# One table set for exp and log, the logarithm summed by TensorE, and two more products per pass on GpSimd, in a bidirectional Mamba layer

## The chip, the cores and the metric

The kernel runs on one core of a Trainium2 chip. The metric is the device time of one execution in microseconds (us). The engines are called as in the profile: PE (TensorE, with PEld for its weight loads), DVE (VectorE), ACT (ScalarE), POOL (GpSimd) and SP (SyncE, which issues most of the DMAs). Each engine takes its instructions in the order in which they were written; between engines semaphores keep the order.

## The reference

One image of 64x64 positions and 256 channels, all in float32. Layer 0 is a convolution block with attention, layer 1 takes the 4096 positions as a sequence: layer norm, a Mamba layer forwards and one backwards, their sum `m`, a layer norm and a small two-layer network on it, and then a mixture of experts. The change lies in the Mamba layers:

```
xz = x @ in_proj.T;  xc, z = split(xz)               # 512 channels each
xc = silu(conv4(xc) + conv_b)
dt, B, C = split(xc @ x_proj.T)                       # 16 columns each
dt = softplus(dt @ dt_proj.T + dt_b)                  # 512 channels
h  = exp(dt * A) * h + dt * B * xc                    # 512 channels x 16 states, along 4096 positions
y  = (sum over states of h * C) + xc * Dp
out = (y * silu(z)) @ out_proj.T
m = fwd + bwd;   t = x1 + m + mlp(layer_norm(m))       # x1 is layer 1's input before its layer norm
```

## The kernel before

The Mamba stage (`mamba_phase`) cuts the 4096 positions into 8 chunks of N = 512 and handles the two directions by turns: 16 *passes*, pass i being chunk i // 2, forwards where i is even and backwards where it is odd. A pass has 32 *slots*, numbered 0 to 31 (`at` in the code): 4 groups of 128 channels (e), 4 groups of states (k) and two halves (j = 0, 2). A slot works on tiles of 128 partitions x 1024. The order of all engines is written out by hand in one loop over 512 slots n (L1979); nothing reorders it.

What a slot n issues, in this order:

- `inflow(n + 2)`, POOL: `dbx` = dt*xc times B (L1890). Three buffers.
- `keep(n - 1)`, ACT: the last column of the states is kept for the next chunk (L1934).
- `decay(n + 1)`, ACT: two Exp of 128x512 into `da` in PSUM (L1880). Two buffers.
- `bring(n + 1)`, ACT or POOL: adds what is carried in from the chunk before.
- `recur(n)`, DVE: the scan along 1024 columns (L1903) in place in `da`, and the product with C (L1908) from `da` to the SBUF tile `h`. Four buffers of `h`. In the slots of the set `POOLED` the scan writes to `h` at once, and POOL does the product in place one slot later (`pooled`, L1913).
- `sum_states`, PE: four matmuls that add up the states of two slots into the PSUM tile `y` (L1943). The pair (n, n + 1) is summed in slot n + 2, or in slot n + 3 where slot n is in `POOLED`. With each new e a matmul for xc * Dp comes first (L1941).
- At slots 0, 8, 16 and 24, `close`, DVE: `y` times silu(z) (L1952).

Beside the slots run *generators*, one step per slot:

- `prepare(q)` makes what pass q needs. It begins in slot 27 of pass q - 2 and lies mostly in pass q - 1: `in_proj` of xc (L1339), the convolution as matmuls with diagonal weights (`taps`, L1385, slots 3 to 6), Silu of xc (slot 8, L1389), the projection to dt, B and C (`wx`, L1394, slot 9), the projection of dt (`wdt`, L1414, slots 11 to 14) with Abs and Relu on ACT, Exp (slot 16, L1417), then in slots 17 to 22 three identity matmuls that add the rounding error, exp(-|.|) and the Relu part (L1430) and a copy by ACT; in slot 23 Ln (L1434) and two matmul groups of z; in slots 24 to 29 and in slots 2 and 4 of the next pass the steps of `dt_piece` on POOL: v = 0 adds Ln to dt (L1458), v = 1 multiplies by xc (L1469) and writes both to DRAM, from where they are read back spread over partitions.
- `output(i - 1)`, slots 1 to 3: the out projection of the pass before (L1527), copied or added into `m`.
- `tail(c)`, one for each chunk but the last: layer norm of `m`, `m + x1` on POOL (L1550), up-projection (L1558), the leaky step (ACT L1562, DVE L1564), down-projection in two halves (L1569, L1574), and another layer norm. Each step names the engine that it needs first, and is taken only in slots that are not in that engine's set in `FULL`. A tail begins in slot 26 of an even pass and ends in slot 25 of the next even pass; the last ends in slot 31 of pass 15. It has one PSUM buffer (`tl_psum`).

The matmul results of `prepare` and `output` share two PSUM buffers (`mm_psum`). ACT needs a table load whenever a function outside the loaded set comes: Silu and Exp do, and Ln was loaded from a set of its own, so a pass has six loads: two for Silu of xc and back, two for Ln and back, two for silu(z) at slot 0 (L2019) and back.

`start()` does for pass 0 what `prepare` does for the others, in part on DVE. After the loop, `ending()` finishes the last chunk.

Of the kernel before, what the change touches and what calls it, by code (L numbers as in the profile page):

```python
# [14 lines left out]
FP = mybir.dt.float32  # L15
# [9 lines left out]
P = 128  # L25
# [1230 lines left out]
def mamba_phase(cx, early, w_in, w_x, w_out, w1, w2, x1d, ud, bcd, dtd, x2d, u2d, usum):  # L1256
# [12 lines left out]
    with ExitStack() as ctx:  # L1269
# [59 lines left out]

        def mm_psum():  # L1330
            return pmm.tile([P, N], FP, name="mm", tag="mm")
# [19 lines left out]
        def in_pair(q, e):  # L1351
            return [in_proj(q % 2, gots[q]["u"], e), in_proj(q % 2, gots[q]["u"], e + 1)]

        def few():
            return sp.tile([P, N], FP, name="few", tag="few", bufs=3)

        def prepare(q):
# [31 lines left out]
            nc.scalar.activation(xc, xc, AF.Silu)  # L1389
            yield  # L1390
            ps = mm_psum()
            nx = DR + 2 * DS
            for e in range(ET):
                nc.tensor.matmul(ps[0:nx, :], wx[d][:, e, :], xc[:, e, :], start=e == 0, stop=e == ET - 1)  # L1394
            yield
            xd = few()[0:nx, :]
            nc.scalar.copy(xd, ps[0:nx, :])

# [7 lines left out]
            for e in range(ET + 1):  # L1406
                if e > 0:
                    ex = early.wide("ex")[:, :, 0:N] if e == 1 else ex
                    dt = dt or sp.tile([P, ET, N], FP, name="dt", tag="dt")
                    nc.scalar.activation(ex[:, e - 1, :], ps, AF.Abs, bias=cx.col(f"dtb{d}", e - 1))  # L1410
                    nc.scalar.activation(dt[:, e - 1, :], ps, AF.Relu, bias=cx.col(f"dtb{d}", e - 1))
                if e < ET:
                    ps = mm_psum()
                    nc.tensor.matmul(ps, wdt[r, P * e : P * e + P], xd[r, :], start=True, stop=True)  # L1414
                yield
# [4 lines left out]
            for e in range(ET + 2):  # L1420
                if e < ET:
                    rd = rds[e] = few()
                    nc.scalar.activation(rd, ex[:, e, :], AF.Identity, scale=-1.0, bias=-1.0)
                    nc.scalar.add(rd, rd, 1.0)
                if e > 1:
                    nc.scalar.copy(dt[:, e - 2, :], sums.pop(e - 2))
                if 0 < e <= ET:
                    ps = sums[e - 1] = mm_psum()
                    for v, x in enumerate((rds.pop(e - 1), ex[:, e - 1, :], dt[:, e - 1, :])):
                        nc.tensor.matmul(ps, cx.ident, x, start=v == 0, stop=v == 2)  # L1430
                yield


            nc.scalar.activation(ex, ex, AF.Ln, bias=1.0)  # L1434
            zs = in_pair(q, ET)
            yield
            got["dt"] = dt
            for at, (v, e) in enumerate(((0, 0), (1, 0), (0, 1), (0, 2), (0, 3), (1, 1))):
                if at == 3 and q > 1:
                    load_first(q, 0)  # L1440
                dt_piece(q, v, e, ex)
                if at in (0, 2):
                    z = sp.tile([P, 2, N], FP, name="z", tag="z", bufs=3)
                    got.setdefault("z", []).append(z)
                if at < 4:
                    nc.scalar.copy(z[:, at % 2, :], zs[at % 2])  # L1446
                if at == 1:
                    zs = in_pair(q, ET + 2)
                    if q + 1 < 2 * NCH:
                        load_u(q + 1)  # L1450
                yield

        def dt_piece(q, v, e, ex=None, eng=nc.gpsimd):


            dt, xc = gots[q]["dt"], gots[q]["xc"]
            if v == 0:
                eng.tensor_tensor(dt[:, e, :], dt[:, e, :], ex[:, e, :], ALU.add)  # L1458
                if q < 2:
                    return  # L1460
                if e == 0:
                    firsts[q] = ip.tile([P, ET], FP, name="first", tag="first", bufs=1)
                nc.gpsimd.tensor_tensor(firsts[q][:, e : e + 1], dt[:, e, 0:1], odd[:, 0:1], ALU.add)
                if e % 2:
                    first_rows[q, e // 2] = cx.rows.tile([P, 2], FP, name="first_row", tag="first_row", bufs=2)
                    nc.sync.dma_start(out=first_rows[q, e // 2], in_=firsts[q][:, e - 1 : e + 1])
            else:
                x = few()
                eng.tensor_tensor(x, dt[:, e, :], xc[:, e, :], ALU.mult)  # L1469

                eng.tensor_tensor(dt[:, e, 0:1], dt[:, e, 0:1], odd[:, 1:2], ALU.add)
                for w, piece in enumerate((dt[:, e, :], x)):
                    nc.sync.dma_start(out=dtd[2 * q + w][e].rearrange("p j n -> (p j) n"), in_=piece)
# [63 lines left out]
        def tail(c):  # L1537
# [3 lines left out]
            yield from layer_norm(cx, tl, tl_psum, m, hn, nc.gpsimd, 2)  # L1541
            x1 = tl.tile([P, CT, N], FP, name="x1", tag="ln_xc")
            nc.sync.dma_start(out=x1, in_=x1d[c])
            for t in range(CT):
                nc.scalar.activation(
                    hn[:, t, :], hn[:, t, :], AF.Identity, scale=cx.col("lng", t), bias=cx.col("lnb", t)
                )
            yield "DMA"
            yield "POOL"
            nc.gpsimd.tensor_tensor(m, x1, m, ALU.add)  # L1550
# [33 lines left out]
        def start():  # L1584
# [10 lines left out]
            nc.scalar.activation(xc, xp[:, :, 0:N], AF.Silu)  # L1595
            for d in range(2):
                nc.scalar.activation(aneg[d], cx.col(f"alog{d}", 0, ET * DS), AF.Exp)

                nc.vector.tensor_scalar(aneg[d], aneg[d], -1.0, -1e-30, ALU.mult, ALU.min)
# [78 lines left out]
            for z in got["z"]:  # L1678
                nc.scalar.activation(z, z, AF.Silu)
            dt_piece(0, 0, 3, ex)  # L1680
# [188 lines left out]
        firsts, first_rows, got_first, brought = {}, {}, {}, {}  # L1869
# [80 lines left out]
        def close(i, e):  # L1950
# [7 lines left out]
        POOLED = {4, 10, 12, 18, 28}  # L1958
# [7 lines left out]
            "PE": {0, 1, 2, 3, 4, 5, 6, 7, 9, 18, 19, 20, 21, 23, 24, 25, 27, 29},  # L1966
            "ACT": {0, 6, 7, 8, 9, 16, 17, 18, 19, 20, 21, 22, 23, 30, 31},
            "POOL": {0, 1, 2, 4, 24, 25, 26, 27, 28, 29, 30, 31},
# [4 lines left out]
        with tc.manual_schedule(engines=ORDERED):  # L1973
# [5 lines left out]
            for n, (i, e, k, j) in enumerate(slots):  # L1979
# [37 lines left out]
                if at == 0 and i > 0:  # L2017
                    for z in gots[i]["z"]:
                        nc.scalar.activation(z, z, AF.Silu)  # L2019
                if i == 0:  # L2020
                    step(begin)
# [4 lines left out]
                if i > 0 and at in (2, 4):  # L2026
                    dt_piece(i, 1, 2 if at == 2 else 3)
# [7 lines left out]
                for _ in range(1 + (i == 2 * NCH - 1 and at in (4, 6, 7))):  # L2035
                    if tails and (i == 2 * NCH - 1 or at not in FULL[needs[0]]):
                        needs[0] = next(tails[0], None)
                        if needs[0] is None:
                            tails.pop(0)
                            needs[0] = "PE"  # L2040
# [358 lines left out]
```

## Time and profile before

| | us |
|---|---|
| median of 3 runs (lowest to highest) | 4099.89 (4095.22 to 4108.44) |
| profiled execution: its time / its span | 4114.01 / 4112.1 |
| Mamba stage in it, first scan to the end of the last slot | 1946.9 to 3819 |
| busy over the span: PE, DVE, ACT, POOL | 3586.2, 3503.9, 2667.8, 1836.6 |
| granted clock of PE over the span | 0.918 |
| passes 2 to 14, scan of slot 0 to the next pass's | 113.5 to 119.8 each |

A line of the groups reads: source line, engine, operation, output <- inputs, shape and count | busy us, mean ns of one | idle time of the engine just before, and what ended most of it. In a timeline a line begins with start and duration in us; the idle time before it stands in brackets. Matmuls of float32 are recorded in two records each. A line of the waits has the waiting instruction, the one that released it, the sum in us, how often, and the longest. A line by stretches has the stretch, its length, the busy time (and count) of PE, PEld, DVE, ACT and POOL, PE's granted clock, the DMA share and GB/s.

### The profile page before, as it was taken

To read this page: it belongs to the slowest core of one execution; us is meant where nothing else is said; L and a number is where in the kernel's file an instruction comes from. 1 tells how busy PE (TensorE), PEld (TensorE's weight loads), DVE (VectorE), ACT (ScalarE), POOL (GpSimd) and SP (SyncE) were. 2 spreads that over 40 slices of the span, in tenths; PEclk is the share of its full clock that TensorE was granted. 3 is DMA by queue.
4 is the path that set the end of the run, shared out by engine and by line. 5 is a ranking of instruction groups with operands and counts; after the bars stand their busy time and mean duration, and the time that the engine had idled before them with its cause. 6 is when DMAs were issued, how large, how long until landed. Compare 5 with 4: busy or idle time off the path is not lost. (4 is left out here: it accounts for less than half of the span.)

```text
span 4112.1 us, 43244 instructions
## 1 busy us (share of the span) xinstructions
PE 3586.2 (87%) x14792; PEld 1183.0 (29%) x14792; DVE 3503.9 (85%) x2919; ACT 2667.8 (65%) x4152; POOL 1836.6 (45%) x1284
## 2 busy tenths in 40 slices
PE   6769888999999999998888788888888888876898
PEld 2324332222222222222222222222223232222444
DVE  8998877989889889877899999999999999999322
ACT  1111226988887878876777777778787777775222
POOL 3020000000000000001888889888888989888100
PEclk9889998999999999998888998898899899888999
DMA  6232215223322223214334344344333434332221
GB/s 208 93 98 95 81 59 157 51 60 65 65 56 62 63 54 65 58 42 122 118 106 129 116 124 130 121 119 129 113 113 119 144 109 133 117 122 90 64 62 55
DMA packets 164324, 399.93 MB, mean 97 GB/s; under 512 B 36997, under 2 KB 46469, under 8 KB 163838
## 3 DMA queue, kind: packets, MB, share of 16 engines
q1 hardware_dynamic: 137166, 304.26, 24.0%
q0 software_dynamic: 24624, 84.43, 8.9%
q10 hardware_dynamic: 2304, 8.39, 0.6%
q8 instruction: 118, 1.93, 0.2%
q14 instruction: 112, 0.92, 0.1%
HBM read 268.17 MB, written 79.56 MB: 85 GB/s over the span
## 5 line engine op out<-in xcount | busy, mean ns | idle before, releaser
L1890 POOL TENSOR_TENSOR dbx<-dtxr,b 128x1024 f32<-128x1024 f32 x512 | 1202.9, 2360 | 201.9 <-DVE da L1903 80.2
L1044 ACT ACTIVATE e<-sc 128x1024 f32<-128x1024 f32 x1024 | 993.8, 1023 | 178.5 <-PE sc L1037 152.7
L1903 DVE TENSOR_TENSOR_SCAN da<-da,state,dbx 128x1024 f32<-128x1024 f32 x432 | 1013.9, 2347 | 16.9 <-ACT da L1880 7.2
L954 DVE TENSOR_TENSOR s<-s,e 128x1024 f32<-128x1024 f32 x768 | 880.5, 1216 | 25.1 <-ACT e L1044 24.4
L1880 ACT ACTIVATE da<-dtr,aneg 128x512 f32<-128x512 f32 x1024 | 708.2, 692 | 33.2 <-DMA dtr<-dtd 3.7
L1037 PE MATMUL sc<-q,kS 32*128 32x512 f32 x4096 | 652.8, 650 | 15.6 <-ACT e L1044 11.4
L961 PE MATMUL av<-e,vT 128*32 128x512 f32 x4096 | 557.2, 612 | 0.4 <-ACT e L1044 0.4
L1908 DVE TENSOR_TENSOR h<-da,c 128x1024 f32<-128x1024 f32 x432 | 529.1, 1225 | 33.2 <-PE y L1943 1.2
L977 POOL DMA_DIRECT2D s<-s x94 | 81.5, 874 | 953.0 <-DVE s L954 901.7
L1943 PE MATMUL y<-h,sel 128*32 128x512 f32 x2048 | 368.9, 654 | 99.2 <-DVE h L1908 74.7
L462 PE MATMUL cv<-v,u 128*128 128x512 f32 x928 | 414.9, 607 | 28.7 <-DVE v L286 13.3
L1037 PEld LDWEIGHTS sc<-q,kS 32*128 32x128 f32 x4096 | 211.5, 185 | 460.0 <-issue 259.4
L1339 PE MATMUL mm<-u,win 128*128 128x512 f32 x464 | 252.8, 695 | 77.1 <-ACT z L1446 25.8
L462 PEld LDWEIGHTS cv<-v,u 128*128 128x128 f32 x928 | 179.4, 195 | 261.9 <-issue 228.4
L560 DVE SCALAR_TENSOR_TENSOR acc<-pad,wdw_s,acc 128x768 f32<-128x768 f32 (+1 forms) x192 | 236.0, 1234 | 19.9 <-ACT acc L553 14.2
L1934 ACT COPY state<-da 128x2 f32<-128x2 f32 x431 | 67.9, 158 | 264.6 <-DVE h L1908 263.5
L1385 PE MATMUL mm<-xp,taps 128*128 128x512 f32 x480 | 212.8, 595 | 0.0
L143 POOL TENSOR_TENSOR ln_few<-ln_few,minus_half 128x4 f32<-128x4 f32 x29 | 34.8, 1201 | 397.5 <-DMA ln_few<-ln_row 259.6
L954 DVE TENSOR_TENSOR s<-e 128x1024 f32<-128x1024 f32 x128 | 151.9, 1217 | 62.2 <-ACT e L1044 53.5
L1903 DVE TENSOR_TENSOR_SCAN h<-da,state,dbx 128x1024 f32<-128x1024 f32 x80 | 187.5, 2344 | 13.0 <-ACT state L1934 11.7
L961 PEld LDWEIGHTS av<-e,vT 128*32 128x32 f32 x4096 | 82.0, 108 | 400.5 <-issue 390.3
L1913 POOL TENSOR_TENSOR h<-h,c 128x1024 f32<-128x1024 f32 x80 | 188.4, 2355 | 1.0 <-ACT state L1934 1.0
(379 smaller groups left out, 3940.9 us busy)
## 6 DMA issues: line engine op xcount, KB each, us to landing
dtr<-dtd SPq DMA_DIRECT2D x128, 512.0 KB
dtxr<-dtd SPq DMA_DIRECT2D x128, 512.0 KB
s<-s POOLq DMA_DIRECT2D x94, 512.0 KB, 5.9
b<-bcd SPq DMA_DIRECT2D x64, 256.0 KB
c<-bcd SPq DMA_DIRECT2D x64, 256.0 KB
dtd<-dt SPq DMA_DIRECT2D x64, 256.0 KB
dtd<-few SPq DMA_DIRECT2D x64, 256.0 KB
u<-uv SPq DMA_DIRECT2D x24, 640.0 KB
```

The costliest lines, as they stand in the source:

```text
L462: nc.tensor.matmul(rows4(ps), u[:, dy, P * ci : P * ci + P], v[:, dy : dy + HR, ci, :], start=dy + ci == 0, stop=dy == k - 1 and ci == CT - 1,
L560: nc.vector.scalar_tensor_tensor(o, src, w_ap, o, ALU.mult, ALU.add)
L954: nc.vector.tensor_tensor(z, x, y, ALU.add)
L961: nc.tensor.matmul(g.av[32 * h : 32 * h + 32, :], vT[:, kb, P * t + 32 * h : P * t + 32 * h + 32], es[h // 2][:, h % 2, :], start=kb == 0, ...
L1037: nc.tensor.matmul(ps[h // 2][:, h % 2, :], kS[r, t, P * kb : P * kb + P], q_t[r, t, :], start=True, stop=True,)
L1044: nc.scalar.activation(e, ps[i], AF.Exp)
L1339: nc.tensor.matmul(ps, win[d][:, t, P * e : P * e + P], u[:, t, ::-1] if d else u[:, t, :], start=t == 0, stop=t == CT - 1,)
L1880: nc.scalar.activation(da[:, v, :], dts[i, e, j][0][:, v, :], AF.Exp, scale=aneg[i % 2][:, a : a + 1])
L1890: nc.gpsimd.tensor_tensor(u, dts[i, e, j][1], bcs[i, k][0][:, None, :].to_broadcast([P, 2, N]), ALU.mult)
L1903: nc.vector.tensor_tensor_scan(das[n].rearrange("p v n -> p (v n)"), da.rearrange("p v n -> p (v n)"), u.rearrange("p v n -> p (v n)"), st ...
L1908: nc.vector.tensor_tensor(h, da, bcs[i, k][1][:, None, :].to_broadcast([P, 2, N]), ALU.mult)
L1943: nc.tensor.matmul(ys[i, e][32 * j : 32 * j + 32, :], cx.sel, hs[n + j // 2][:, j % 2, :], start=False, stop=k == SQ - 1,)
```

## The change

- ACT loads the set that holds Exp and Ln together after each Silu (`exp_and_log`), so Ln needs no load: four loads per pass.
- Ln is taken in four parts (`logs`). The sum of dt in PSUM stays open after its three identity matmuls, and a fourth adds Ln. ACT copies the finished sum (`keep_dt`) and, for the carry, its first column. The v = 0 steps on POOL go, but for `start()`; the four v = 1 steps lie in slots 21, 23, 25 and 27.
- The four projections of z go from slots 23 and 25 to slots 9, 10, 19 and 21, their copies to 10, 11, 20 and 22.
- The tail adds x1 to `m` by two identity matmuls for each half and a copy by ACT, within the waits of its first layer norm, instead of on POOL.
- `POOLED` is {0, 4, 8, 12, 16, 20, 28} instead of {4, 10, 12, 18, 28}.
- `FULL` is changed. By the order of the new instructions a tail now begins in slot 8 of an even pass and ends in slot 30 of the next odd pass: up-projections in slots 23, 25, 28 and 30 of the even pass, the two halves of the down-projection in slots 8 and 10 of the odd one. The last ends in slot 17 of pass 15.

```diff
+        def exp_and_log():
+            nc.scalar.preload_act_table_set("natural_log_exp_and_others")
...
             nc.scalar.activation(xc, xc, AF.Silu)
+            exp_and_log()
             yield
...  (wx)
+            z_of(q, 0)
             yield
             xd = few()[0:nx, :]
             nc.scalar.copy(xd, ps[0:nx, :])
+            keep_z(q, 0)
+            z_of(q, 1)
...  (Exp)
+            def keep_dt(e):
+                nc.scalar.copy(dt[:, e, :], sums[e])
...
+                nc.scalar.copy(firsts[q, h][:, e % 2 : e % 2 + 1], sums[e][:, 0:1])
...
+            rounding(0)
+            yield
+            for e in range(ET + 1):
+                if e > 0:
+                    keep_dt(e - 1)
                 if e < ET:
-                    rd = rds[e] = few()
...
+                    total(e)
+                if e < ET - 1:
+                    rounding(e + 1)
+                if 0 < e < 3:
+                    keep_z(q, e + 1)
                 yield
-            nc.scalar.activation(ex, ex, AF.Ln, bias=1.0)
-            zs = in_pair(q, ET)
...
+                if e < ET:
+                    logs(e)
+                    if e < 2:
+                        z_of(q, e + 2)
+                    nc.tensor.matmul(sums[e], cx.ident, ex[:, e, :], start=False, stop=True)
+                if e > 0:
+                    dt_piece(q, 1, e - 1)
...
                 yield
...  (tail)
-            yield from layer_norm(cx, tl, tl_psum, m, hn, nc.gpsimd, 2)
-            x1 = tl.tile([P, CT, N], FP, name="x1", tag="ln_xc")
+            x1 = tl.tile([P, CT, N], FP, name="x1", tag="a1b")
             nc.sync.dma_start(out=x1, in_=x1d[c])
+            for need in layer_norm(cx, tl, tl_psum, m, hn, nc.gpsimd, 2):
...
+                if waits > 1:
+                    nc.scalar.copy(m[:, waits - 2, :], ps)
+                if waits < 3:
+                    ps = tl_psum()
+                    nc.tensor.matmul(ps, cx.ident, m[:, waits - 1, :], start=True, stop=False)
+                    nc.tensor.matmul(ps, cx.ident, x1[:, waits - 1, :], start=False, stop=True)
...
-            nc.gpsimd.tensor_tensor(m, x1, m, ALU.add)
...
-        POOLED = {4, 10, 12, 18, 28}
+        POOLED = {0, 4, 8, 12, 16, 20, 28}
...
-            "PE": {0, 1, 2, 3, 4, 5, 6, 7, 9, 18, 19, 20, 21, 23, 24, 25, 27, 29},
-            "ACT": {0, 6, 7, 8, 9, 16, 17, 18, 19, 20, 21, 22, 23, 30, 31},
-            "POOL": {0, 1, 2, 4, 24, 25, 26, 27, 28, 29, 30, 31},
+            "PE": {1, 2, 3, 4, 5, 6, 7, 9, 18, 20, 21, 22, 24, 27, 29},
+            "ACT": {0, 6, 7, 8, 9, 14, 15, 16, 20, 22, 30, 31},
+            "POOL": {1, 5, 9, 13, 17, 21, 23, 25, 27, 29, 30, 31},
...
                     for z in gots[i]["z"]:
                         nc.scalar.activation(z, z, AF.Silu)
+                    exp_and_log()
...
-                if i > 0 and at in (2, 4):
-                    dt_piece(i, 1, 2 if at == 2 else 3)
...
-                for _ in range(1 + (i == 2 * NCH - 1 and at in (4, 6, 7))):
+                if tails and (i == 2 * NCH - 1 or at not in FULL[needs[0]]):
...
```

## The prediction

> **What bounds the kernel now.** I read the page's groups first, then the busy times by stretch, the DVE's waits, and the timelines of single slots. "Slot" and "pass" are as in the section on the kernel; times inside a pass are starts of the 512 rows of L1903.
>
> ```profile
> L1890 POOL TENSOR_TENSOR dbx<-dtxr,b 128x1024 f32<-128x1024 f32 x512 | 1202.9, 2360 | 201.9 <-DVE da L1903 80.2
> L1903 DVE TENSOR_TENSOR_SCAN da<-da,state,dbx 128x1024 f32<-128x1024 f32 x432 | 1013.9, 2347 | 16.9 <-ACT da L1880 7.2
> L1908 DVE TENSOR_TENSOR h<-da,c 128x1024 f32<-128x1024 f32 x432 | 529.1, 1225 | 33.2 <-PE y L1943 1.2
> L1913 POOL TENSOR_TENSOR h<-h,c 128x1024 f32<-128x1024 f32 x80 | 188.4, 2355 | 1.0 <-ACT state L1934 1.0
> ```
>
> The Mamba stage runs from the first scan (1946.9) to 3819. By stretches, DVE is busy 1791 of these 1872 us, POOL 1629, PE 1552, ACT 1425: DVE sets the pace. A slot whose product is on DVE lasts 3.52 to 3.59 us from scan to scan; with the product on POOL 2.26:
>
> ```profile
> 2511.61 2.35 DVE L1903 TENSOR_TENSOR_SCAN h<-da,state,dbx 128x1024 f32<-128x1024 f32 x1
> 2513.87 2.33 DVE L1903 TENSOR_TENSOR_SCAN da<-da,state,dbx 128x1024 f32<-128x1024 f32 x1
> 2516.24 1.23 DVE L1908 TENSOR_TENSOR h<-da,c 128x1024 f32<-128x1024 f32 x1
> 2517.38 2.35 DVE L1903 TENSOR_TENSOR_SCAN da<-da,state,dbx 128x1024 f32<-128x1024 f32 x1
> ```
>
> The DVE's little idle time is of two kinds, PE late with sums, ACT late with decays:
>
> ```profile
> DVE xc L1952 <- PE y L1943: 14.3, 8, 2.5
> DVE h L1903 <- ACT state L1934: 11.7, 13, 1.6
> ```
>
> Slot 0 (here starting at 2524.6) shows the second limit. ACT's queue is decay, load, Silu, state, load, decay; the scan of slot 2 follows 8.07 us after that of slot 0:
>
> ```profile
> 2524.88 1.42 ACT L1880 ACTIVATE da<-dtr,aneg 128x512 f32<-128x512 f32 x2
> 2526.31 1.28 ACT L2019 ACT_TABLE_LOAD   x1
> 2527.61 2.00 ACT L2019 ACTIVATE z<-z 128x1024 f32<-128x1024 f32 x2
> 2529.52 0.14 ACT L1934 COPY state<-da 128x2 f32<-128x2 f32 x1
> 2529.68 1.28 ACT L1880 ACT_TABLE_LOAD   x1
> 2530.97 1.42 ACT L1880 ACTIVATE da<-dtr,aneg 128x512 f32<-128x512 f32 x2
> 2532.32 0.28 ACT L1928 ACTIVATE dbx<-dbx,brought 128x1 f32<-128x1 f32 x1
> ```
>
> Slot 8, with the Silu of xc, is the same chain: 7.98. And the PE timeline shows what happens after a gap: eight records of L1569 take 6.76 us, the next eight (L1394) 3.63.
>
> ```profile
> 2901.87 2.88 PE L1943 MATMUL y<-h,sel 128*32 128x512 f32 x16
> 2908.55 3.78 PE L1569 MATMUL tl<-a1a,w2s 128*128 128x512 f32 x4 [3.79 <-DVE m L1574]
> 2912.12 3.18 PE L1569 MATMUL tl<-a1b,w2s 128*128 128x512 f32 x4
> 2915.23 3.63 PE L1394 MATMUL mm<-xc,wx 128*48 128x512 f32 x8
> ```
>
> **The sum.** It is made against the profiled execution (4114.0, span 4112.1). That run is 14.1 above the median of 4099.9, and I add the difference to the median.
>
> *Content of DVE.* Five products per pass on POOL become seven: 2 x 16 = 32 fewer on DVE, at 3.53 - 2.26 = 1.27 each: **-40.6** if nothing else comes last. Where is each of them?
>
> *Slot 0.* Nothing in ACT's chain there gets shorter: the joint set's load stands where the load for Exp stood. So slot 2 still starts at 8.07, while DVE now needs 2.26 + 0.68 (the close) + 3.52 = 6.46. Before, slots 0 and 1 took 8.4 on the mean against a content of 7.7. The wait grows by 0.9 in 15 passes: **+13**; most of this product buys nothing.
>
> *Slots 8 to 12.* Slots 8 and 12 replace 10 and 12, so the content is the same, but slot 10 can't start before 7.98 either. The new thing is in PE's order. A pair of slots whose first is on POOL is summed one slot later, in the third slot after it (L2002), and a scan on a POOL slot writes the h buffer of four slots before by itself, so it waits for that sum; a DVE slot writes it 2.4 us later, by the product. With 0, 4, 8, 12, 16 and 20 on POOL each such scan has one slot of slack. In odd passes of the new order, PE has before the sum of slot 8: the tail's first down-projection (which waits for the leaky step on DVE, at 2.26 + 0.68 + 0.66 = 3.6), wx, two projections of z, the second down-projection, the skip product. From slot 8's scan: 3.6 + 6.76 (the L1569 row above, half clock) + 3.63 + 3.6 + 3.6 (eight records of L1339 took 3.60) + 0.96 + 0.5 = 22.7. DVE could go at 7.98 + 3.52 + 0.66 + 3.52 = 15.7, its content alone is 14.8. So 7.9 of waiting, where the odd passes had 1.0 (14.5 against 13.5): 6.9 in the six odd passes 3 to 13: **+41**. At full clock (3.6 for the first eight) it is 3.2 less for each, +22; that is the lower bound. PE's gap ahead of this chain is 2.4 us (its sums end 1.2 after slot 8's scan, as in the rows above). I take the half clock because a shorter gap shows it: after one of 1.76 us before 2569.74 the granted clock (the number before the last two) was 0.50:
>
> ```profile
> 2570.00:2576.80 6.80, 6.80 (x14) 1.67 (x6) 6.59 (x5) 5.14 (x12) 6.80 (x4) 0.50 0.60 192
> ```
>
> The Trainium skill, "TensorE: Matmul & The Clock Gate", Part 1, says the clock halves after an idle window of about 3.4 us; by that alone a 2.4 us gap keeps full clock and the sum would end 19 lower, but this row speaks against it.
>
> Even passes have a mean before the gap: wx at full or half clock gives 15.0 to 16.9, where they took 16.0: between -1.0 and +0.9 with another tail step inside, taken as **+1** in all. Passes 0 and 1: **+3** (POOL is packed in the first slots, and pass 1 had no wait here).
>
> *Slot 16.* 16 replaces 18: no change of content. But in odd passes slots 16 to 20 took 15.3 against 13.5, since the close waited for PE, held by the up-projections of slots 13 and 15. These now lie in slots 23 to 30: **-11**. The new tail work there (x1's two sums, the second waiting for ACT's copy at slot 14) has the sum of slot 12 queued behind it, with 1.8 us to spare.
>
> *Slot 20.* Here the seventh product really shortens the content. But ACT has keep 0.16, decays 1.42, bring 0.2, copy of dt 0.48, its first column 0.15, rounding 1.14, z 0.48: 4.0 us in a slot of 2.26, and again in slot 22. The decays for 23 and 24 come 0.3 (odd) to 0.9 (even, with the tail's two scalings) late: **+9** over 15 passes. PE has 26 us of matmuls in the 28 us of slots 18 to 25, and each logarithm matmul waits for ACT's Ln with the next slot's sums queued behind it; in even passes an up-projection stands before the sum that slot 24's close needs: 0.8 x 7 = **+6**.
>
> *Start and end.* The load of 1.28 us between Abs and Exp (at 1932.6) is on the way to the first scan: **-1.3**. The last tail ends at slot 17 of pass 15 instead of 31, so about 2.5 of that pass's 4 us of waits go: **-2.5**.
>
> *Off the path.* ACT: 34 loads fewer at 1.283 (-44); four logarithms for one +0.4 x 15, first columns +8, copies of m +7. At slot 23, where the old Ln and its loads stood, DVE waited only 0.1 us, so these loads were covered; if they were not, their ceiling would be 30 x 1.28. The skill's "ScalarE: Activation LUTs", What ACT_TABLE_LOAD costs, adds a drain of 1.38 us to each: by it ACT would gain 90. The rows show none: decays end at 2609.74 and the load starts at 2609.76. The sum doesn't change either way. POOL: -71 (dt + ex) -11 -16 (x1) +75 (32 products of 2.355) = -23; its dt pieces come before they did, so no load is later. PE: 60 logarithm matmuls and 28 for x1 at 0.9, +79, in 320 us of gaps; the cost of where they stand is in the terms above. On SP as many transfers are issued as before; x1 is loaded a layer norm earlier and the first columns after ACT instead of POOL; no reader is near: 0.
>
> Sum: -40.6 + 13 + 41 + 1 + 3 - 11 + 9 + 6 - 1.3 - 2.5 = **+18**: 4132 for such a profile, 4117 for the median.
>
> **Rivals.** *The sums come in time (0.30).* If PE passes slots 8 to 12 without holding the scan, the +41 falls away, and the +9 and +6 shrink by half: -31, 4069. For it: DVE's waits for PE are only some 19 us now, and PE's queue slips work into gaps that I can only count on average. Against: PE is in order, and one buffer ring of four leaves no way round. It decides as soon as the sum of slot 8 ends within 15.7 us of slot 8's scan.
>
> *Full clock (0.23).* The same wait at 3.2 less: -1, 4099: no change that can be told. A measurement of this kernel tells about 0.3% (12 us) from nothing.
>
> *TensorE becomes the bound (part of the slower case).* If the packed slots 18 to 25 run partly at half clock, with each odd or even pass losing one more 1.7 us: +27 on top, 4144. For: clock 0.88 in this stage. Against: fewer gaps there, since z no longer waits at slot 23.
>
> That the joint set might not take effect is no rival: the new order has 64 loads in the stage where the old has 98.
>
> **Numbers.** The likeliest case is the slower one, 0.47 with TensorE's worse variant: 4117, alone from 4108 to 4144. Range 4066 to 4142: from the first rival to near the upper bound. Over 0.3% faster 0.30, within 0.23, slower 0.47.
>
> **What would show it.** In the profile after: the scan's wait for PE y should grow from 0.4 us to about 45, in six long waits of 5 to 8, all at slot 12 of odd passes; slot 0 to 2 still 8.07; slots 20 to 24 near 13.6 (now 14.4); slots 16 to 20 of odd passes 13.5. The step on the down-projection is wrong if that wait is under 10 us in all; the one on ACT if slot 2 follows slot 0 in under 7.5. Wrong as a whole would be a time under 4088.

## The result: slower by one per cent, and the profile after

| | before | after |
|---|---|---|
| median of 4 runs each, us (lowest to highest) | 4104.2 (4095.2 to 4112.7) | 4144.1 (4133.3 to 4158.5) |
| ratio after / before, 95% interval | | 1.0097 (1.0076 to 1.0117) |
| profiled execution: time / span, us | 4114.0 / 4112.1 | 4158.5 / 4156.7 |
| Mamba stage, first scan to last scan, us | 1868.8 | 1908.5 |
| busy over the span: PE, DVE, ACT, POOL, us | 3586, 3504, 2668, 1837 | 3615, 3470, 2644, 1822 |

The forecast was 4117 with 4142 as its upper end. The sign was right, and so was the largest wait; the time lay 2 us above the upper end. Of the 27 us between 4117 and 4144, 4 are in the base: the forecast was added to the median of three runs, 4099.9, and with the fourth the kernel before has 4104.2.

The groups of the scan, the product and `dbx`, after (columns as in the section on the profile before):

```profile
L1928 POOL TENSOR_TENSOR dbx<-dtxr,b 128x1024 f32<-128x1024 f32 x512 | 1204.7, 2361 | 233.8 <-DVE h L1941 99.9
L1941 DVE TENSOR_TENSOR_SCAN da<-da,state,dbx 128x1024 f32<-128x1024 f32 x400 | 939.4, 2348 | 46.4 <-ACT state L1972 14.9
L1946 DVE TENSOR_TENSOR h<-da,c 128x1024 f32<-128x1024 f32 x400 | 489.9, 1225 | 28.0 <-PE mm L1423 1.4
L1941 DVE TENSOR_TENSOR_SCAN h<-da,state,dbx 128x1024 f32<-128x1024 f32 x112 | 262.5, 2344 | 67.2 <-PE y L1981 57.7
L1951 POOL TENSOR_TENSOR h<-h,c 128x1024 f32<-128x1024 f32 x112 | 264.1, 2358 | 32.4 <-ACT state L1972 32.3
```

The product fell from 529.1 to 489.9 us on VectorE: the 39 us that 32 products are worth did go. The right-hand column shows what came instead. In front of the scans on POOL slots (112 of them) VectorE now stands idle for 67 us, 57.7 of it for the sums on TensorE. The same group before had 13.0 in all, and 0.4 of it for the sums:

```profile
L1903 DVE TENSOR_TENSOR_SCAN h<-da,state,dbx 128x1024 f32<-128x1024 f32 x80 | 187.5, 2344 | 13.0 <-ACT state L1934 11.7
```

The products on POOL (last line of the groups after) now wait 32.3 us for `state`, the copy that `keep` makes on ACT; before they waited 1.0.

VectorE's waits from 1940 to 3860, after (waiting instruction, releaser, sum in us, times, longest):

```profile
DVE h L1941 <- PE y L1981: 57.7, 26, 5.8
DVE da L1941 <- ACT state L1972: 14.9, 17, 1.7
DVE xc L1990 <- PE y L1981: 13.4, 9, 4.2
DVE da L1941 <- ACT dbx L1966: 10.8, 14, 1.7
DVE da L1941 <- POOL dbx L1964: 9.6, 5, 2.9
DVE da L1941 <- ACT da L1918: 9.0, 12, 2.0
```

Pass 7 around slots 8 to 12, TensorE first (start, duration, groups of records; idle time before in brackets). The scan of slot 8 starts at 2808.54:

```profile
2812.18 3.52 PE L1605 MATMUL tl<-a1a,w2s 128*128 128x512 f32 x4 [2.44 <-DVE a1b L1600]
...
2817.35 3.63 PE L1398 MATMUL mm<-xc,wx 128*48 128x512 f32 x8
2820.91 3.70 PE L1342 MATMUL mm<-u,win 128*128 128x512 f32 x8
2824.45 1.88 PE L1605 MATMUL tl<-a1a,w2s 128*128 128x512 f32 x4
2826.17 1.88 PE L1605 MATMUL tl<-a1b,w2s 128*128 128x512 f32 x4
2827.88 1.02 PE L1979 MATMUL y<-xc,skip 128*128 128x512 f32 x2
2828.84 1.06 PE L1981 MATMUL y<-h,sel 128*32 128x512 f32 x8
```

And VectorE:

```profile
2823.14 1.23 DVE L1946 TENSOR_TENSOR h<-da,c 128x1024 f32<-128x1024 f32 x1
2830.01 2.35 DVE L1941 TENSOR_TENSOR_SCAN h<-da,state,dbx 128x1024 f32<-128x1024 f32 x1 [5.64 <-PE y L1981]
```

That is the order of the forecast to the letter: down-projection, wx, z, z, down-projection, skip, sum; then the scan of slot 12. The six odd passes 3 to 13 each have one such wait of 5.6 to 5.8 us.

Where the 44.6 us between the two spans lie, by the starts of the scans, against the sum of the forecast taken apart in the same way:

| part | forecast | measured |
|---|---|---|
| up to the first scan | -1.3 | +1.5 |
| passes 0 and 1 | about -0.5 | +5.0, +2.7 |
| even passes 2 to 14 | about 0 | +10.4 |
| odd passes 3 to 13 | +24 | +25.9 |
| pass 15 | -3.5 | -4.4 |
| behind the last scan | 0 | +3.4 |

So the odd passes came as forecast, and the even passes and pass 0 are the miss. (Behind the last scan one close waits 4.3 us for its sum; before, one waited 1.2.) One caution on small terms: in the profiles of all kernels of this study the first scan starts between 1932.2 and 1954.7 us, although nearly all that lies ahead of it is the same code. The Mamba stage, from first to last scan, is the finer measure, and is given below beside the times.

### The profile page after: what moved, and what is told of

It is laid out like the page before. It is cut to its first block, busy times and chain, and to the rows that moved or that the text cites. A ratio compares the mean times of both kernels' runs of the same rounds, so it can differ in the third digit from the quotient of the medians.

```text
span 4156.7 us, 43587 instructions
## 1 busy us (share of the span) xinstructions
PE 3614.8 (87%) x14968; PEld 1207.3 (29%) x14968; DVE 3469.6 (83%) x2887; ACT 2644.1 (64%) x4233; POOL 1821.6 (44%) x1193
## 5 line engine op out<-in xcount | busy, mean ns | idle before, releaser
L1941 DVE TENSOR_TENSOR_SCAN da<-da,state,dbx 128x1024 f32<-128x1024 f32 x400 | 939.4, 2348 | 46.4 <-ACT state L1972 14.9
L1946 DVE TENSOR_TENSOR h<-da,c 128x1024 f32<-128x1024 f32 x400 | 489.9, 1225 | 28.0 <-PE mm L1423 1.4
L1981 PE MATMUL y<-h,sel 128*32 128x512 f32 x2048 | 346.6, 648 | 104.1 <-DVE h L1946 72.6
L1941 DVE TENSOR_TENSOR_SCAN h<-da,state,dbx 128x1024 f32<-128x1024 f32 x112 | 262.5, 2344 | 67.2 <-PE y L1981 57.7
L1951 POOL TENSOR_TENSOR h<-h,c 128x1024 f32<-128x1024 f32 x112 | 264.1, 2358 | 32.4 <-ACT state L1972 32.3
L1342 PE MATMUL mm<-u,win 128*128 128x512 f32 x464 | 234.7, 647 | 30.2 <-ACT xp L1370 27.9
L560 DVE SCALAR_TENSOR_TENSOR acc<-pad,wdw_s,acc 128x768 f32<-128x768 f32 (+1 forms) x192 | 236.0, 1234 | 19.9 <-ACT acc L553 14.2
```

What stands on the lines that cost most here:

```text
L560: nc.vector.scalar_tensor_tensor(o, src, w_ap, o, ALU.mult, ALU.add)
L1941: nc.vector.tensor_tensor_scan(das[n].rearrange("p v n -> p (v n)"), da.rearrange("p v n -> p (v n)"), u.rearrange("p v n -> p (v n)"), st ...
L1946: nc.vector.tensor_tensor(h, da, bcs[i, k][1][:, None, :].to_broadcast([P, 2, N]), ALU.mult)
L1951: nc.gpsimd.tensor_tensor(hs[n], hs[n], bcs[i, k][1][:, None, :].to_broadcast([P, 2, N]), ALU.mult)
L1981: nc.tensor.matmul(ys[i, e][32 * j : 32 * j + 32, :], cx.sel, hs[n + j // 2][:, j % 2, :], start=False, stop=k == SQ - 1,)
```

## The experiments

Theory 1 is the one of the forecast: a product on POOL is worth its 1.27 us on VectorE, but the scan in such a slot writes the buffer of `h` itself and waits for a sum of four slots before, and what stands ahead of that sum in TensorE's queue decides. The rivals: the waits only move (TensorE or ACT have no room); the new order costs by itself; the table loads matter.

### The down-projections behind the sum of slot 8

```diff
a_w2b:
-            "PE": {1, 2, 3, 4, 5, 6, 7, 9, 18, ...
+            "PE": {1, 2, 3, 4, 5, 6, 7, 9, 10, 18, ...
a_w2ab:
-                if tails and (i == 2 * NCH - 1 or at not in FULL[needs[0]]):
+                if tails and (i == 2 * NCH - 1 or at not in FULL[needs[0]]
+                              and not (i % 2 and needs[0] == "PE" and at in (8, 10))):
```

> The changed kernel, with the second down-projection of the tail issued in slot 11 (behind the sum of slot 8) and no longer in slot 10. Theory 1 (the scan of slot 12 waits for the sum of slot 8, which stands in TensorE's queue behind wx, two z projections and both down-projections): the sum comes 3.6 us earlier, the six waits of 5.8 us shrink to about 2.2, so 6 x 3.6 = 21.6 us less than the changed kernel's 4144: 4122, and VectorE's wait for PE y in L1941 falls from 57.7 to about 36. Theory 2 (TensorE has no room; what is taken from one place in its queue is missing at the next sum): less than 8 us gained, the wait turns up at slots 13 to 16.

> The changed kernel, with both down-projections behind the sum of slot 8 in odd passes (slots 11 and 13 instead of 8 and 10). Theory 1: the six waits of 5.8 us go, 34.8 us less: 4109, odd passes 115.6 us instead of 121.4. Theory 2 (TensorE has no room): less than 12 us gained, and the sums of slots 10 and 12 come late in place of that of slot 8.

One half moved: 4123.4 (1.0048 of before, 1.0031 to 1.0065), 20.6 less than the changed kernel, where 21.6 was expected; the wait for PE y fell to 29.3 us, the longest to 2.4. Both moved: 4118.4 (1.0030, 1.0012 to 1.0047), 25.7 less; odd passes 116.7 instead of 121.4. In a_w2ab:

```profile
DVE h L1941 <- PE y L1981: 19.0, 13, 1.8
```

The long waits are gone. Of the 34.8 us expected 9 came back: slots 16 to 20 of the odd passes went from 13.7 to 15.5 us, since the steps of x2 (VectorE adds each half of the down-projection to `m`, L1610), and what else the tail had there, come later. The forecast's step on the down-projection stands, with its size.

### The last up-projection behind the sum of slot 28

```diff
-            "PE": {..., 24, 27, 29},
+            "PE": {..., 24, 27, 29, 30},
```

> The changed kernel, with the tail's last up-projection issued in slot 31, behind the sum of slot 28, and no longer in slot 30. Theory 1: the same mechanism acts in even passes: slot 0 is now a POOL slot, so its scan writes the buffer of slot 28 and waits for that sum; five idle stretches of 1.1 to 2.3 us at the end of even passes (7.2 us together) go: 4137. Theory 2 (this wait is of no account, even passes are longer for another reason): 4144 within 4 us.

4148.7 (1.0110, 1.0092 to 1.0128): nothing gained. The even passes did get shorter, 117.2 instead of 118.3, slots 28 to 32 of them 14.3 instead of 15.4; but the odd passes went from 121.4 to 123.4, mostly in slots 0 to 2 (9.6 instead of 7.4) and 4 to 8. In each of the six odd passes the close in slot 0 now waits 2.8 to 3.4 us (18.6 in all) for its sum, which stands behind the moved up-projection: TensorE itself waits there for VectorE's leaky step (5.0 us in front of pass 9). Theory 1 had the right wait and the wrong worth; the wait was moved to the next sum.

### The products alone, the new order alone, and without slots 0 and 8

```diff
b_pool7 (kernel before):     -POOLED = {4, 10, 12, 18, 28}            +POOLED = {0, 4, 8, 12, 16, 20, 28}
a_pool5 (changed kernel):    -POOLED = {0, 4, 8, 12, 16, 20, 28}      +POOLED = {4, 10, 12, 18, 28}
a_no08_w2ab (a_w2ab):        -POOLED = {0, 4, 8, 12, 16, 20, 28}      +POOLED = {4, 12, 16, 20, 28}
```

> The kernel before, with the seven products on POOL (slots 0, 4, 8, 12, 16, 20, 28) as its only change. Theory 1 (two of the seven stand in slots that ACT's chain of decay, Silu and load bounds, and slot 0 then waits for the sum of slot 28 behind a down-projection): 40.6 us of VectorE's work go, about 19 come back at slots 0, 1 and 9 and about 14 at the end of odd passes: 4096 against 4104. Theory 2 (the products are worth their work): 4063. Theory 3 (POOL with seven products falls behind with dbx): 4120 or more.

> The changed kernel with the old five products on POOL (slots 4, 10, 12, 18, 28): the new order of the preparation and of the tail without the two added products. Theory 1 (the products on POOL make the waits, the new order alone is about neutral): VectorE gets 40.6 us more work, but the waits of 34.8 us at slot 12, about 7 at slot 31 and about 13 behind ACT's chain at slots 0 and 1 go: 4104 to 4130. Theory 3 (the products are worth their 40 us, and the new order itself costs 80): 4170 to 4185.

> The changed kernel with both down-projections behind the sum of slot 8, as before in a_w2ab (4118), and without the products of slots 0 and 8 on POOL (five: 4, 12, 16, 20, 28). Theory 1 (the products in slots 0 and 8 buy little, since ACT's chain bounds these slots, and make scans wait for sums): 40.6 us more of VectorE's work, about 14 x 3.4 = 48 us less of waiting at slots 0, 1, 7 and 9: 4110. Theory 2 (they are worth their work): 4118 + 40 = 4158.

| | us | ratio to before | stage, us |
|---|---|---|---|
| b_pool7 | 4125.8 | 1.0045 (1.0029 to 1.0060) | 1889.2 |
| a_pool5 | 4146.3 | 1.0100 (1.0084 to 1.0117) | 1911.5 |
| a_no08_w2ab | 4133.6 | 1.0073 (1.0046 to 1.0100) | 1900.5 |

None came as theory 1 said. b_pool7 has the time of theory 3 (4120 or more), but not its cause: VectorE waited 11.0 us for POOL's `dbx` there, against 5.2 before, and 52.5 for sums (25.3 before scans, 27.2 before closes), against 15.9. The seven products by themselves make the old order slower: 20 us in the stage, although 40 us of work leave VectorE. The old five in the new order are no better than the seven. Taking the products of slots 0 and 8 away costs 15 of the 40 us that they hold: between the theories.

The traces show a reason common to the three; I call it the moved wait. In a_pool5 slot 18 lasts 4.04 us instead of 2.26 in every pass from 2 to 14, in b_pool7 slots 16 to 20 of the even passes 6 to 14 take 16.1 where passes 2 and 4 take 14.2, in a_no08_w2ab slot 12 of odd passes 4.04. In each of them ACT starts the decay for the next slot just as the scan of the POOL slot ends, 2.38 us after that scan's start; in nearly all other POOL slots it starts at most 0.6 us after the start, beside the scan. The compiled programs show the difference: in these slots `keep` has no wait for VectorE of its own; the decay ahead of it in ACT's queue has one that covers it. Nothing in the source asks the decay to wait for that scan; why the compiled program puts the wait there was not settled. It stands in slot 18 of passes 2 to 14 and slot 12 of odd ones in a_pool5, in slot 16 of the even passes 6 to 14 in b_pool7, in slot 12 of odd passes in a_no08_w2ab. By the slots' lengths, 5 x 1.9 = 10 us of b_pool7, 13 x 1.8 = 23 of a_pool5 and 6 x 1.8 = 11 of a_no08_w2ab are this. Without it (an estimate; no such program was run) they would be at some 4116, 4123 and 4123. In the kernel before and in the changed one it stands in pass 0 alone, at slots 12 and 18 and at slots 8, 12 and 16. So it explains little of the forecast's miss, but these three runs can't be read as plain sums.

In slot 12 of a_pool5's odd passes the moved wait adds nothing, since VectorE stands there for TensorE in any case. These are its two largest waits in slots 10 to 13 of the six odd passes:

```profile
DVE h L1941 <- ACT dbx L1966: 20.6, 6, 3.6
DVE m L1610 <- PE tl L1605: 16.9, 8, 2.5
```

In the first, ACT's decay and `dbx` for slot 12 stand in its queue behind the copies of the results of wx and z, which TensorE makes behind the first half of the down-projection; in pass 7 ACT idled 3.67 us for wx and 1.33 for z. The second is x2's step, waiting for the second half (2.5 us in each of the six). So the new order of TensorE costs some 35 us in these passes with the old five products too, though no scan waits for a sum there: the rival that the new order costs by itself is right for this place.

### A sixth product, and the moved wait seen

b_two and b_six start from b_joint_up (below).

```diff
b_six:  -POOLED = {4, 10, 12, 18, 28}   +POOLED = {4, 10, 12, 18, 20, 28}
b_two:  -POOLED = {4, 10, 12, 18, 28}   +POOLED = {2, 4, 10, 12, 18, 28}
```

> b_joint_up with one more product on POOL, at slot 20 alone (six: 4, 10, 12, 18, 20, 28). Slot 20 has no Silu in ACT's queue, and the sum of slot 16 that its scan waits for is issued in slot 18, two slots ahead. Theory 1 (a product on POOL is worth its 1.27 us where neither ACT's chain nor a sum one slot ahead stands behind it): 16 x 1.27 = 20 us less than b_joint_up, 4075 to 4080, slots 20 to 24 at 13.0 to 13.1 instead of 14.4. Theory 3 (POOL is full there, with a product every second slot from 18): under 5 us gained.

> b_joint_up (4098) with a sixth product on POOL, in slot 2, where ACT's work in the slot (keep, decay, bring: 1.9 us, in odd passes 2.4) about fits the shortened slot of 2.26 us, and no matmul that waits stands between the sums and their scans. Theory 1 (a product on POOL is worth its 1.27 us where ACT's work fits the slot and the sum comes in time): 16 x 1.27 = 20 us less work on VectorE, some 6 us back because POOL has only 1.8 to 2.8 us to spare around slots 0 to 3: 4084. Theory 3 (POOL is full with six): dbx comes late at slots 4 to 7, 4095 to 4105.

b_six: 4109.3 (1.0003, 0.9991 to 1.0014), slower than b_joint_up. ACT and VectorE in slot 20 of b_six, pass 6; the scan of slot 20 runs from 2722.89 to 2725.23:

```profile
2723.47 0.59 ACT L1427 COPY dt<-mm 128x512 f32<-128x512 f32 x1 [0.42 <-PE mm L1431]
2723.95 0.17 ACT L1937 COPY state<-da 128x2 f32<-128x2 f32 x1
2725.27 1.42 ACT L1883 ACTIVATE da<-dtr,aneg 128x512 f32<-128x512 f32 x2 [1.15 <-DVE h L1906]
2726.62 0.28 ACT L1931 ACTIVATE dbx<-dbx,brought 128x1 f32<-128x1 f32 x1
```

```profile
2722.89 2.34 DVE L1906 TENSOR_TENSOR_SCAN h<-da,state,dbx 128x1024 f32<-128x1024 f32 x1
2726.93 2.36 DVE L1906 TENSOR_TENSOR_SCAN da<-da,state,dbx 128x1024 f32<-128x1024 f32 x1 [1.70 <-ACT dbx L1931]
```

`dbx` by ACT is named as the releaser, but the loss is one line up: the decay stood 1.15 us for the end of the scan beside which it should have run. Slots 20 to 24 took 14.83 (the median of passes 2 to 14), and slot 20 alone 4.04 instead of 2.26; less these 1.78 it would be the 13.05 that theory 1 gave. That nothing was gained is also what theory 3 forecast, but VectorE's waits for POOL's `dbx` were 1.3 us here, against 8.0 in b_joint_up, so POOL was not full.

b_two: 4099.4 (0.9985, 0.9973 to 0.9998), the same as b_joint_up. It has no moved wait behind pass 0, and slot 2 shrank as expected (slots 2 to 4: 7.0 and 5.8 instead of 8.25 and 7.06). The even passes kept 1.0 of the 1.27; the odd ones gave all of it back in slots 4 to 8 (14.3 instead of 13.1), mostly at slot 7. VectorE's wait for ACT's `dbx` rose from 7.9 to 13.9 us, that for POOL's `dbx` fell from 6.3 to 4.7. But ACT is only the last link: its step on `dbx` itself waits for POOL's, 36.2 us from 1930 to 3830 where b_joint_up has 18.1, and from slot 4 to slot 8 of pass 7 POOL works without a gap. So POOL was the bound there, and theory 3 had the place and the time (4095 to 4105).

### Five buffers for h

```diff
a_h5, a_h5_w2ab:
-        bcp = ctx.enter_context(tc.tile_pool(name="c_bc", bufs=5))
+        bcp = ctx.enter_context(tc.tile_pool(name="c_bc", bufs=4))
-        hp = ctx.enter_context(tc.tile_pool(name="c_h", bufs=4))
+        hp = ctx.enter_context(tc.tile_pool(name="c_h", bufs=5))
a_bc4: the first of the two alone
```

> The changed kernel with five buffers for h instead of four, and four instead of five for each of b and c to make room. A scan on a POOL slot now writes the buffer of five slots before, whose sum is issued well ahead. Theory 1 (the scans wait because the ring of four gives the sum one slot): the wait of L1941 for PE y falls from 57.7 us to under 15, and some 6 x 2 us come back at slot 12 as the wait of x2's step for the second down-projection: 4144 - 43 + 12 = 4113. Theory 2 (TensorE's lateness is what counts, whoever waits for it): the wait moves to x2's step, the close and ACT's reads of dt, less than 12 us gained.

> The same five buffers for h, with both down-projections behind the sum of slot 8 as in a_w2ab (4118). Theory 1: the remaining 19 us of L1941's wait for PE y go, ACT's chains at slots 0 and 8 stay: 4100 to 4108. Theory 2 (they are replaced by other waits): 4118 within 5.

> The changed kernel with four buffers instead of five for each of b and c and nothing else: what made room in a_h5 (4189). Theory 1 (a_h5 was slow for want of the b and c buffers; the fifth buffer of h took the waits away that the changed kernel has): slower than a_h5 by the 30 to 45 us of waits for sums, 4220 to 4235. Theory 2 (the fifth buffer of h brings nothing, the waits only move): 4189 within 8. Theory 4 (the b and c buffers cost nothing, and the fifth buffer of h itself makes the kernel slow): 4144.

| | us | ratio to before | even, odd passes, us |
|---|---|---|---|
| a_h5 | 4189.3 | 1.0207 (1.0185 to 1.0230) | 121.9, 122.7 |
| a_h5_w2ab | 4183.8 | 1.0188 (1.0169 to 1.0207) | 122.1, 121.9 |
| a_bc4 | 4197.0 | 1.0238 (1.0211 to 1.0266) | 120.3, 126.6 |

The first two missed badly, and a_bc4 says why: the fifth buffer of b and c is worth 53 us of the changed kernel. The waits that grew in a_bc4 are VectorE's for `dbx`: 39.8 us for POOL's step on it (9.6 in the changed kernel), 26.4 for ACT's before scans on POOL slots (2.8). Its time is the one that theory 2 gave (4189 within 8), but the ring of five does what theory 1 said at the place itself. First a_bc4, then a_h5:

```profile
DVE h L1941 <- PE y L1981: 62.7, 29, 6.4
```

```profile
DVE h L1941 <- PE y L1981: 1.1, 1, 1.1
```

Slots 10 to 12 of odd passes fell from 13.4 to 7.7, and moving the down-projections, worth 25.7 us with four buffers, is worth 5.5 with five. So with these seven products the down-projections cost mainly through the ring of `h`. In total only 7.7 us were won, and the largest loss seen is the moved wait, which a_h5 has in slot 8 of passes 1 to 14: slots 8 to 10 take 10.1 instead of 7.4 to 7.9 us, some 2.4 in each, 34 in all. a_h5_w2ab has it too. These 2.4 us may also give TensorE time to catch up, so without them the down-projections could cost more than the 5.5.

### The table set, the slot 16 wait, and both

```diff
b_joint:     +nc.scalar.preload_act_table_set("natural_log_exp_and_others")   (behind each Silu)
b_up:        -"PE": {..., 7, 9, 18, ...   +"PE": {..., 7, 9, 15, 18, ...
b_joint_up:  both
```

> The kernel before, with the joint table set loaded behind each Silu as its only change (about 30 table loads fewer in the Mamba stage). Theory 1 (these loads lay beside other work): within 4 us of the kernel before. Theory 2 (the loads are on the path): 30 x 1.28 = 38 us less, 4066.

> The kernel before, with the tail's second up-projection in slot 16, behind the sum of slot 14, and no longer in slot 15. My step on slot 16 (the close there waits 1.5 to 2.2 us in six odd passes for TensorE, held by this up-projection): 11.2 us of idle time go, about 10 less: 4094. Against it: the work is only moved, and the close or the scan at slots 17 to 20 waits in its place: within 4 us of 4104.

> The kernel before with the joint table set and with the second up-projection in slot 16, the edits of b_joint (4101) and b_up (4102) together. If the two gains are separate: 7 + 5.5 us less than the 4107.6 of the runs of before, 4095. If both shorten the same wait (the close of slot 16 in odd passes, 15.3 us from slot 16 to 20 before, 14.0 and 14.2 with either): 4100.

| | us | ratio to before | stage, us |
|---|---|---|---|
| b_joint | 4100.6 | 0.9986 (0.9971 to 1.0000) | 1860.1 |
| b_up | 4102.1 | 0.9987 (0.9973 to 1.0001) | 1858.4 |
| b_joint_up | 4097.7 | 0.9984 (0.9973 to 0.9994) | 1863.7 |

The loads were covered, as forecast: not 38 us. What little b_joint won lies in slots 16 to 20 of odd passes, 14.0 instead of 15.3, which is where b_up won 7 of its 10.4 us of the stage (14.15); together they win that wait once. b_joint_up is the one of these whose interval lies below one: 0.16% faster than before, and so faster than both kernels of this case.

### x1 on POOL again

```diff
-                if waits > 1:
-                    nc.scalar.copy(m[:, waits - 2, :], ps)
-                if waits < 3:
-                    ps = tl_psum()
-                    nc.tensor.matmul(ps, cx.ident, m[:, waits - 1, :], start=True, stop=False)
-                    nc.tensor.matmul(ps, cx.ident, x1[:, waits - 1, :], start=False, stop=True)
+                if waits == 3:
+                    nc.gpsimd.tensor_tensor(m, x1, m, ALU.add)
```

> a_w2ab (4118) with x1 added by POOL in one instruction, as in the kernel before, instead of by TensorE's four matmuls and ACT's two copies, in the same slot. Theory 1 (in even passes the second of these sums waits for ACT's copy with the sum of slot 12 queued behind it, and the scan of slot 16 waits: 1.5 us at slot 15 in five even passes): about 8 us less, 4110. Theory 2 (these waits have another cause): 4118 within 4.

4118.8 (1.0042, 1.0026 to 1.0058) against 4118.4: no gain. The wait of 1.5 us at slot 15 went from all even passes, so its cause was as said. But slots 20 to 24 of these passes grew from 13.3 to 15.3 us, and VectorE's wait for the `dbx` that POOL finishes grew from 11.0 us in a_w2ab to this in a_w2ab_x1:

```profile
DVE da L1937 <- POOL dbx L1960: 20.2, 13, 3.4
```

## Why the prediction was too low

**Right, with its size.** The 40.6 us of VectorE's work (39.2 in the group). The odd passes: +24 forecast, +25.9 measured, with the wait at slot 12 in all six and its cause shown by a_w2b and a_h5. That the sum fits so well is partly luck. VectorE's idle time in slots 8 to 12 grew by 35.3 us, not 41, and in slots 0 to 2 by 0.3, not 5; slots 20 to 24 and 28 to 32 took 7.4 us more than their terms, and 9.4 us of work left these passes where the sum has 15.2. In detail, the first half of the down-projection took 5.2 to 5.4 us, not 6.76, and the sum of slot 8 ended 21.4 us after that slot's scan, not 22.7. Slot 16: -9.9 over the six odd passes for -11. The ACT term of slot 20: slots 20 to 24 took 13.6 and 14.5 for a content of 13.1, 11.6 us in 13 passes for +9 in 15. Slot 24: the idle time grew by 8 us for +6. The table loads: covered. Off the path, ACT's busy time changed by -24 us for -23, POOL's by -15 for -23, and PE's by +29 for +79; no term of the time rests on these.

**Right at the place, but not by its own test.** Slot 2 was to follow slot 0 in 8.07 us. It took 8.6 in even passes and 7.4 in odd ones, where the scan of slot 0 itself comes late and ACT's chain has begun before it. In the odd passes that is under the 7.5 that the prediction named as its sign of being wrong. VectorE's idle time in slots 0 and 1 grew by 12 us over the 15 passes, for +13, but 11 of them lie in the even passes, and most of those have another cause (below): the size is luck, the chain as the only reason is wrong.

**The step that failed** is the sum's account of the even passes and of passes 0 and 1. The even passes 2 to 14 measured +10.4 where the terms come to nothing, passes 0 and 1 +7.8 where they come to -0.5: 19 of the 26 us missing between the two profiles; 6 more lie before the first and behind the last scan. The "+1 in all" is not the term that was short: it is for slots 8 to 12 of the even passes alone, and these became 7.7 us shorter. VectorE's idle time in the seven even passes grew like this, against the terms for the same slots:

| slots | forecast, us | measured, us |
|---|---|---|
| 0 to 2 | +6.1 | +11.0 |
| 8 to 12 | +1 | -7.7 |
| 12 to 16 | 0 | +6.7 |
| 20 to 24 | +4.2 | +2.1 |
| 24 to 28 (the close of slot 24) | +6 | +8.4 |
| 28 to 32 | 0 | +6.7 |
| the others | 0 | +2.4 |
| sum | +17.3 | +29.6 |

So waits that the sum put at nothing, or too low, are the miss:

- The rule that I priced at slot 12 holds at every POOL slot, and slots 0 and 16 were new ones. The scan of slot 0 waits for the sum of slot 28, behind the last up-projection (five even passes, 1.0 to 2.2 us each at the end of slot 31; three of them end with that sum, two with ACT's decay); that of slot 16 for the sum of slot 12, behind x1's second sum, which waits for ACT's copy (four even passes, 1.1 to 1.4 at the end of slot 15). For the first the sum has no term; for the second I had written 1.8 us to spare.
- The operand of slot 1 comes late. In five even passes the scan of slot 1 itself waits 1.0 to 2.9 us for POOL's `dbx`, 9.6 in all (the line of L1964 above); before, one even pass did, 1.4. POOL makes this `dbx` only when its `dtxr` has been read back from DRAM: in all seven even passes it waited 1.6 to 3.6 us for that transfer, and before, in five of them, 3.2 to 4.7. Counted from the scan of slot 0, POOL now starts on it after 1.5 us on the mean of these passes, where it was 0.4, and slot 0 itself is 1.3 us shorter. The forecast had put the transfers at 0 ("no load is later"). Why they land later was not tested.
- One wait that grew costs nothing here. The product on POOL runs in place, so it waits for ACT's `keep`. In slots 0 and 8 `keep` stands behind Silu and a table load, and POOL's next `dbx` behind the product. ACT, then POOL, in slot 8 of pass 7 in the changed kernel:

```profile
2811.59 1.91 ACT L1392 ACTIVATE xc<-xc 128x2048 f32<-128x2048 f32 x1
2813.51 1.28 ACT L1331 ACT_TABLE_LOAD   x1
2814.81 0.19 ACT L1972 COPY state<-h 128x2 f32<-128x2 f32 x1
```

```profile
2815.08 2.35 POOL L1951 TENSOR_TENSOR h<-h,c 128x1024 f32<-128x1024 f32 x1 [1.76 <-ACT state L1972]
2817.39 2.35 POOL L1928 TENSOR_TENSOR dbx<-dtxr,b 128x1024 f32<-128x1024 f32 x1
```

  The scan had ended at 2810.88; the product could start at 2815.08. Waits like this one, most of them for the product of slot 8, are the 32.3 us of the last group line above; a_no08_w2ab has 5.3. But they are idle time of POOL: in passes 1 to 14 VectorE waits for no `dbx` of POOL except the five at slot 1.
- In pass 0, where `start()` still prepares, VectorE waited 5.5 us for POOL's `dbx` in front of the scans of slots 4, 5 and 8, and 2.7 for the sum in front of that of slot 20; neither was there before. The pass took 119.9 to 122.8 us in the kernels with the old five products, 124.2 to 129.1 with the seven (125.0 in the changed kernel), but 125.2 with the five of a_no08_w2ab, so the number of products alone does not set it. Pass 1 got the wait at slot 12 too (2.1 us). VectorE's idle time in the two passes grew by 11.9 us, where "Passes 0 and 1: +3" and their shares of slots 0 and 20 make 4.5.

Yet a_w13 and a_w2ab_x1 each took one of these waits away and won nothing. So the even passes' 10 us are not the price of one place. What the two runs show is that the place next in line was as late: in a_w13 the close of slot 0 behind the moved up-projection, in a_w2ab_x1 the `dbx` of ACT and POOL in slots 20 to 24. Which change would win them is open, and the late `dtxr` at slot 1 was not tried. The rival "the sums come in time" fell at once; "full clock" is in between, since TensorE ran at half clock for the first half of the down-projection only; TensorE as the bound of slots 18 to 25 gave 4144 too, but that is chance: its place was not there, and those slots cost what the likeliest case had for them.

## What to carry to other kernels

When work moves off the busiest engine in some slots, list for each of these slots everything that now has a shorter time to arrive: the sum that frees the buffer, the copy that must come before an in-place step, the operand of the slot after; a mechanism found at one slot is to be priced at all of them. Where one engine is busy 96% of a stage and three others over 75%, a wait removed alone is mostly replaced by the next one, so try removals together or expect a part. And before a run with one set changed is read as "that part alone", look whether its waits stand in the same instructions: here a wait that the compiled program had put one step earlier in ACT's queue was worth 1.8 us per slot. Idle time that grew on an engine is a loss only where the busiest engine waits for what it makes, and the named releaser may itself have waited for another: follow it one step further.

## What the runs showed of the hardware that I had not expected

- TensorE's slow stretch after a gap was short. In pass 7 of the changed kernel, after 2.44 us of idle time, the first four records of the down-projection took 3.52 us and the last four of the second half 1.88; the granted clock was 0.50 from 2812.20 to 2815.00 and 1.00 from 2815.60 to 2817.30. The first eight records took 5.2 to 5.4 us in all six odd passes. The Trainium skill, "TensorE: Matmul & The Clock Gate", Part 1, has the clock halved after an idle window of about 3.4 us; here 2.44 us of idle time were enough, for some 3 us, and the measurement decides.
- Nearly the same code ahead of the Mamba stage took from 1932.2 to 1954.7 us in the profiles, more than most of the differences studied; the stage itself can be compared more finely.
- One buffer less for b and c (five to four) cost 53 us of the changed kernel, more than any other single edit here.
